# A transformer block with routed experts on one core: the second product of an expert block one block later, and two edits to the planner's steps

## The chip, the cores and the metric

The kernel runs on one core of a Trainium2 chip. The core has five engines that work side by side, each through its own queue of instructions in program order: TensorE (PE; its weight loads are shown as PEld), VectorE (DVE), ScalarE (ACT), GpSimd (POOL) and SyncE (SP, here a queue that issues DMAs). Instructions on different engines wait for each other by semaphores. The metric is the device time of one execution in microseconds (us); smaller is better.

## What is computed

The input is x of shape 2 x 2048 x 256 in fp32, that is two batches of 2048 tokens. Four stages are added to it in turn, each on the layer-normed x:

```python
x = x + attention(layernorm(x))     # 16 heads, causal
x = x + moe(layernorm(x))           # first round, f = 0
x = x + mixer(layernorm(x))
x = x + moe(layernorm(x))           # second round, f = 1, same weights

# moe: 8 experts, the best 2 of each token, and a shared expert for all
h = silu(xt @ w1e.T + b1e) * (xt @ w3e.T + b3e)      # per expert, 256 wide
out_e = h @ w2e.T + b2e
y = sum over the token's two experts of gate * out_e
z = silu(xt @ ws1.T + bs1) * (xt @ ws3.T + bs3) @ ws2.T + bs2   # 512 wide

# mixer
delta = softplus(x @ W1.T + b1)
y = x * delta * ((x @ W2.T + b2) . (x @ W3.T + b3))
```

## The kernel before, in words

**Two halves.** The first half (up to about 1120 us) is attention with a schedule written out by hand. The change does not touch it. The second half holds both rounds of the mixture of experts and the mixer between them. Its tokens are cut into 8 chunks of 512 (c = 0 to 7, four for each batch b), and x stays in SBUF in one tile per chunk.

**Routed experts.** `route` (L744) norms a chunk, transposes it and scores the experts. `sort` (L805) gives each of a batch's 4096 pairs of token and expert a slot, so that tokens of one expert lie together in blocks of 128 rows; there are always EB = 39 blocks for each round and batch. `scatter` (L892) writes the normed rows into the DRAM tile XS at these slots with 32 indirect DMAs issued by POOL (L901). `routed` (L1047) then runs the blocks. `combine` (L916) gathers the results from the DRAM tile YS with 8 indirect DMAs of POOL for each chunk (L928), and DVE adds them, weighted, into x (L941). In the second round a chunk that is complete is written out (L950).

**A run of blocks.** There are four runs of `routed`, one for each round f and batch b. In a run a block j goes through these functions:

- `load(j)` (L1065): SP brings the block's 128 rows from XS into a tile `xs` (four buffers).
- `turn(i)` (L1070): PE transposes two things into one PSUM bank: the activated block i (`es`) and the loaded block i + 4 (`xs`). ACT copies the bank to a tile `turned` (L1083, three buffers).
- `up(j)` (L1085): PE makes the first product `eu` of block j from `turned[j-4]`; DVE adds the bias into `ea` (L1098); ACT takes silu of one half into `es` (L1100).
- `gate(j)` (L1103): DVE multiplies `es` by the other half of `ea` (L1106).
- `down(j)` (L1109): PE makes the second product `ed` from `turned[j]` (L1117); DVE adds the bias into `ey` (L1123, two buffers); SP stores it to YS (L1124).

The loop at L1138 joins them. In iteration i it issues `up(i + 1)`, `down(i - 2)`, `turn(i - 1)`, `load(i + 7)` and `gate(i + 1)`. Calls outside 0 to EB - 1 do nothing.

**Shared expert.** `shared(f, c)` (L1008) takes a chunk through the first two products (`s`, L1019, 16 matmul instructions), silu on ACT (L1021), a multiply on DVE (L1024), the third product (`sy`, L1036, 16 instructions) and an add into x on DVE (L1042).

**Mixer.** `mixer(c)` (L954) norms and transposes a chunk, multiplies by the joined weights (`psz`, L969) and builds softplus from an absolute value (L981), an exponential (L982), an add on POOL (L984), a logarithm on ACT (L992) and several steps on DVE and POOL.

**PSUM.** The banks `ab` (four, for `eu`, the transposes of `turn`, and `s`), `py` (two, for `ed` and `sy`) and `px` (two, for the other transposes, routing and mixer).

**The planner.** The order of all this on each engine is fixed when the program is built. Every work function is a generator. It yields a step as a tuple of estimated costs in us for (DVE, ACT, PE, POOL) around the instructions that it issues. The loop at L1222 takes turns between two main streams, one run of `routed` ("experts") and one chunk of `shared` ("share"), one step each. It adds a step's PE cost to the plan's clock `free[2]`, and the other costs to the clocks of their engines. After each main step `beside()` (L1186) issues steps of three side streams, `moving` (scatters and combines), `mixing` (mixers) and `routing`, as long as the engines that a side step needs are planned to be free within a lead (LEAD, L1181) of the PE clock and its own predecessor is planned to be done (AHEAD). So a side step's place depends on the PE time that the main steps claim.

In a mixer and in the other side streams the tuple yielded comes before the instructions that it stands for; in `routed` and `shared` it comes after them.

A run of experts starts when its scatter is planned to be through (`placed`). A shared chunk starts when its transposed input is there and one of two things holds: all XTS = 3 tiles for transposed inputs are in use, or no expert run is open or ready:

```python
            wait = "experts" in mains or (todo and todo[0] in placed)
            if fit and (live[0] >= XTS or not wait):
```

Of the kernel before, what the change touches and what calls it, by code (L numbers as in the profile page):

```python
# [35 lines left out]
EB = (TOPK * N + E * (P - 1)) // P  # L36
# [15 lines left out]
def hybrid_block(  # L52
# [87 lines left out]
    with tc.tile_pool(name="aw", bufs=1) as aw, ExitStack() as aw_ctx:  # L140
# [109 lines left out]
        with ExitStack() as ac:  # L250
# [303 lines left out]
            while na < len(units) or due or behind:  # L554
# [12 lines left out]
                if run_m:  # L567
# [13 lines left out]
                    kc, i = mx.pick(cols)  # L581
# [108 lines left out]
    def side_bank(nm):  # L690
        return ps_x.tile([P, CH], F32, tag="px", name=nm)
# [8 lines left out]
    def feature_major(nm):  # L700
        while live[0] >= XTS:
            yield None
        live[0] += 1
        return cw.tile([P, 2, CH], F32, tag="xT", name=f"xT_{nm}", bufs=XTS)

    def token_major(nm):
        while held[0] >= XNS:
            yield None
        held[0] += 1
        return cw.tile([P, NB, D], F32, tag="xn", name=f"xn_{nm}", bufs=XNS)  # L710
# [23 lines left out]
    def flipped(xn, xT, nm):  # L734
        yield (0, 1.2, 0.9, 0)
        for d in range(2):
            ps = side_bank(f"flip_{nm}_{d}")
            for i in range(NB):
                nc.tensor.transpose(
                    ps[:, i * P:(i + 1) * P], xn[:, i, d * P:(d + 1) * P], ident  # L740
                )
            nc.scalar.copy(xT[:, d, :], ps)
# [211 lines left out]
    def mixer(c):  # L954

        while c not in joined or (0, c) not in added:
            yield None
        xc = X[c]
        xn = yield from token_major(f"b{c}")
        yield from normed(xc, xn, f"b{c}")  # L960
        xT = yield from feature_major(f"b{c}")
        yield from flipped(xn, xT, f"b{c}")
        z = cw.tile([P, NB, NZ], F32, tag="z", name=f"z_{c}")
        for i in range(NB):
            if i % 2 == 0:
                yield (0.9, 0, 2.0, 0)
            ps = side_bank(f"psz_{c}_{i}")
            for d in range(2):
                nc.tensor.matmul(  # L969
                    ps[:, :NZ], xT[:, d, i * P:(i + 1) * P], wz_s[:, d, :],  # L970
                    start=d == 0, stop=d == 1,
                )
            nc.vector.tensor_add(z[:, i, :], ps[:, :NZ], bz_s)
        live[0] -= 1
        zz = z[:, :, 0:D]


        t = cw.tile([P, NB, D], F32, tag="spt", name=f"spt_{c}")
        u = cw.tile([P, NB, D], F32, tag="spu", name=f"spu_{c}")
        yield (0, 2.0, 0, 0)  # L980
        nc.scalar.activation(t, zz, AF.Abs)  # L981
        nc.scalar.activation(t, t, AF.Exp, scale=-1.0)  # L982
        yield (0, 0, 0, 1.3)
        nc.gpsimd.tensor_scalar_add(u, t, 1.0)  # L984
        bcm = small.tile([P, NB, NS], F32, tag="bcm", name=f"bcm_{c}", bufs=2)
        bc = small.tile([P, NB], F32, tag="bc", name=f"bc_{c}", bufs=2)
        yield (1.5, 0, 0, 0)
        nc.vector.tensor_mul(bcm, z[:, :, D:D + NS], z[:, :, D + NS:])
        nc.vector.reduce_sum(bc, bcm, axis=AX.X)
        nc.vector.scalar_tensor_tensor(t, u, 1.0, t, ALU.subtract, ALU.subtract)  # L990
        yield (0, 1.0, 0, 0)
        nc.scalar.activation(u, u, AF.Ln)  # L992
        yield (0, 0, 0, 2.5)
        nc.gpsimd.tensor_tensor(u, u, t, ALU.subtract)
        yield (1.2, 0, 0, 0)
        nc.vector.scalar_tensor_tensor(u, zz, 0.0, u, ALU.max, ALU.add)
        yield (0, 0, 0, 2.5)
        nc.gpsimd.tensor_tensor(xn, xn, u, ALU.mult)
        for h in range(2):
            yield (1.0, 0, 0, 0)  # L1000
            for i in range(2 * h, 2 * h + 2):
                nc.vector.scalar_tensor_tensor(
                    xc[:, i, :], xn[:, i, :], bc[:, i:i + 1], xc[:, i, :], ALU.mult, ALU.add
                )
        mixed.add(c)
        held[0] -= 1
# [40 lines left out]
    def routed(f, b):  # L1047

        xs, turned, h, reg = {}, {}, {}, {}
        nm = f"{f}_{b}"  # L1050
        ws = {
            e: [
                nc.values_load(
                    words[f, b][0:1, w:w + 1], engines=[e], min_val=0, max_val=8 ** FW - 1,
                    skip_runtime_bounds_check_because="words of eight experts",
                )
                for w in range(WORDS)
            ]
            for e in (mybir.EngineType.PE, mybir.EngineType.DVE)
        }  # L1060

        def expert(j, eng):
            return (ws[eng][j // FW] >> (3 * (j % FW))) & (E - 1)

        def load(j):  # L1065
            if j < EB and j not in xs:
                xs[j] = ew.tile([P, D], F32, tag="xs", name=f"xs_{nm}_{j}", bufs=4)
                nc.sync.dma_start(xs[j], XS[b][j * P:(j + 1) * P, :])

        def turn(i):  # L1070

            halves = [t for t in ((h.pop(i, None), 0), (xs.pop(i + 4, None), 1)) if t[0] is not None]
            if not halves:
                return
            ps = ps_ab.tile([P, 2, D], F32, tag="ab", name=f"tr_{nm}_{i}")
            for t, k in halves:
                for d in range(2):
                    nc.tensor.transpose(  # L1078
                        ps[:, k, d * P:(d + 1) * P], t[:, d * P:(d + 1) * P], ident
                    )  # L1080
            turned[i] = ew.tile([P, 2, D], F32, tag="turned", name=f"turned_{nm}_{i}", bufs=3)
            a, z = halves[0][1], halves[-1][1] + 1
            nc.scalar.copy(turned[i][:, a:z, :], ps[:, a:z, :])  # L1083

        def up(j):  # L1085
            if j >= EB:
                return
            v = expert(j, mybir.EngineType.PE) * WE
            o = expert(j, mybir.EngineType.DVE) * BE
            ps = ps_ab.tile([P, CH], F32, tag="ab", name=f"eu_{nm}_{j}")  # L1090
            t = turned[j - 4]
            for d in range(2):
                nc.tensor.matmul(  # L1093
                    ps, t[:, 1, d * P:(d + 1) * P], we_s[:, bass.ds(v + d * CH, CH)],
                    start=d == 0, stop=d == 1,
                )
            a = ew.tile([P, CH], F32, tag="ea", name=f"ea_{nm}_{j}", bufs=2)
            nc.vector.tensor_add(a, ps, be_s[:, bass.ds(o, CH)])  # L1098
            t = ew.tile([P, D], F32, tag="es", name=f"es_{nm}_{j}", bufs=3)
            nc.scalar.activation(t, a[:, 0:D], AF.Silu)  # L1100
            h[j] = (t, a)

        def gate(j):  # L1103
            if j < EB:
                t, a = h[j]
                nc.vector.tensor_tensor(t, t, a[:, D:], ALU.mult)  # L1106
                h[j] = t

        def down(j):  # L1109
            if j < 0:  # L1110
                return
            v = expert(j, mybir.EngineType.PE) * WE
            o = expert(j, mybir.EngineType.DVE) * BE
            ps = ps_y.tile([P, CH], F32, tag="py", name=f"ed_{nm}_{j}")
            t = turned[j]
            for d in range(2):
                nc.tensor.matmul(  # L1117
                    ps[:, 0:D], t[:, 0, d * P:(d + 1) * P],
                    we_s[:, bass.ds(v + 2 * CH + d * D, D)],
                    start=d == 0, stop=d == 1,  # L1120
                )
            y = ew.tile([P, D], F32, tag="ey", name=f"ey_{nm}_{j}", bufs=2)
            nc.vector.tensor_add(y, ps[:, 0:D], be_s[:, bass.ds(o + CH, D)])  # L1123
            nc.sync.dma_start(YS[b][j * P:(j + 1) * P, :], y)  # L1124

        for j in range(4):
            load(j)
        yield (0, 0, 2.5, 0)
        for j in range(4):
            turn(j - 4)  # L1130
            load(j + 4)
            if j == 1:
                yield (0, 0.8, 0.5, 0)
                up(0)
                yield (0.7, 0.45, 1.72, 0)
        yield (0.4, 0.9, 0.5, 0)
        gate(0)
        for i in range(EB + 2):  # L1138
            up(i + 1)
            yield (0.7, 0.45, 1.72, 0)  # L1140
            down(i - 2)
            if i > 0:
                turn(i - 1)
            load(i + 7)
            yield (0.4, 0.6, 1.3, 0)
            gate(i + 1)
            yield (0.42, 0, 0, 0)
        ran.add((f, b))


# [23 lines left out]
    def mixing():  # L1174
        for c in range(TC):
            yield from mixer(c)
# [141 lines left out]
```

## Time and profile before

The time is the median of 3 runs. The profile is one execution by itself; its span is from its first to its last instruction.

| what | value |
|---|---|
| time, median of 3 runs | 2194.92 us (2192.74 to 2195.27) |
| profiled execution, its own time | 2195.39 us |
| its span | 2193.7 us |
| mean granted clock of TensorE | 0.964 |
| scatters (32 indirect stores of POOL, first to last) | from 1212.6, 1320.9, 1669.7 and 1946.4 us, some 42 to 45 us each |
| last second product `ed` of the program | 2139.2 to 2140.3 us |
| first and last gather behind it | 2143.5 and 2187.4 us (end of the last) |

How it is read: a row of a group or of the timeline names the line of the kernel, the engine, the operation and its tiles (out<-in), how often, and how long. "idle before" is the time in which the engine had nothing to run just before that instruction, with the one that released it. "remote" stands for an unknown releaser. In the timeline the first two columns are start and duration in us, and neighbouring instructions of one kind are merged. A stretch's row gives the busy time of each engine in it. PE counts each matmul of the program as two records here.

### The profile page before, as it was taken

How to read it: one execution, taken by the hardware profiler on the slowest of the kernel's cores; microseconds unless marked ns; L12 is line 12 of the kernel's file. 1: busy time of each engine (PE TensorE's matmuls, PEld its weight loads, DVE VectorE, ACT ScalarE, POOL GpSimd, SP SyncE). 2: the span in 40 equal slices, each digit the busy share in tenths (PEclk: the TensorE clock that was granted, in tenths of full speed). 3: DMA queues.
4: the chain of work that ended last, by engine and by line, in shares of the span. 5: the costliest groups of instructions: out<-in, count | busy, mean ns of one | idle time of the engine just before them, and what ended most of it. 6: DMA issues, size and time to landing. Idle time of an engine off the chain costs nothing.

```text
span 2193.7 us, 36069 instructions
## 1 busy us (share of the span) xinstructions
PE 2018.5 (92%) x11840; PEld 1077.3 (49%) x11840; DVE 1358.3 (62%) x3428; ACT 1064.1 (49%) x1566; POOL 870.1 (40%) x1153
## 2 busy tenths in 40 slices
PE   6999999999999999999989995999998799987993
PEld 4444444444444444444446563656664456654662
DVE  4767776777667777678515462447775277652643
ACT  1567477577767677678851121323442144421330
POOL 3434344254344444344451716025235352343305
PEclk8999999999999999999999997999999899998997
DMA  3211110000000000000013212233101241012523
GB/s 95 72 39 57 33 32 7 8 6 4 9 4 6 4 4 6 4 4 1 3 53 160 80 49 92 87 100 98 58 25 68 74 121 61 22 63 75 178 79 120
DMA packets 87602, 113.03 MB, mean 52 GB/s; under 512 B 16384, under 2 KB 75136, under 8 KB 87296
## 3 DMA queue, kind: packets, MB, share of 16 engines
q1 hardware_dynamic: 73488, 75.08, 10.8%
q0 software_dynamic: 12288, 33.57, 4.6%
q8 instruction: 101, 1.65, 0.3%
q10 hardware_dynamic: 1648, 2.10, 0.3%
q14 instruction: 77, 0.63, 0.1%
HBM read 54.59 MB, written 51.64 MB: 48 GB/s over the span
## 4 chain that ended last, share of the span: by engine, by line
PE 79%; DVE 6%; issue 4%; another core or an unknown queue 4%; ACT 3%; POOL 2%; DMA 1%; DVEq 0%; SPq 0%; ACTq 0%; POOLq 0%
PE st L394 15%; PE o L413 12%; PE psm L344 12%; PE eu L1093 10%; PE s L1019 8%; PE ed L1117 5%; PE sy L1036 4%; PE psk L278 3%; PE tr L1078 2%; PE psv L304 1%; PE psj L462 1%; PE psz L969 1%; PE psl L769 1%; POOL yg L928 1%
## 5 line engine op out<-in xcount | busy, mean ns | idle before, releaser
L398 ACT ACTIVATE pt<-st 128x1024 f32<-128x1024 f32 (+3 forms) x640 | 551.9, 896 | 177.3 <-PE psm L344 130.6
L344 PE MATMUL psm<-kT,qT 32*128 32x512 f32 (+3 forms) x2560 | 611.0, 564 | 8.6 <-DMA kT<-sk 4.2
L394 PE MATMUL st<-qT,kT 32*128 32x512 f32 (+3 forms) x2560 | 592.1, 554 | 3.0 <-ACT pt L398 2.9
L358 DVE TENSOR_REDUCE part<-psm 128x1 f32<-128x512 f32 x768 | 478.3, 683 | 148.9 <-PE psm L344 144.0
L424 POOL TENSOR_TENSOR oa<-oa,op 128x512 f32<-128x512 f32 (+3 forms) x288 | 313.5, 1089 | 408.2 <-ACT op L422 406.3
L394 PEld LDWEIGHTS st<-qT,kT 32*128 32x128 f32 x2560 | 251.1, 184 | 214.6 <-ACT pt L398 137.8
L344 PEld LDWEIGHTS psm<-kT,qT 32*128 32x128 f32 x2560 | 272.2, 185 | 84.9 <-issue 33.0
L413 PE MATMUL o<-pt,v 128*32 128x512 f32 (+3 forms) x2560 | 301.5, 541 | 12.9 <-DVE part L358 5.5
L353 DVE CUSTOM_DVE_ANT_0 junk<-psm,maskq 128x512 bf16<-128x512 f32 (+3 forms) x512 | 224.1, 487 | 76.5 <-PE psm L344 58.9
L1093 PE MATMUL eu<-we,turned 128*128 x560 | 264.8, 595 | 0.0
L1100 ACT ACTIVATE es<-ea 128x256 f32<-128x256 f32 x156 | 65.0, 417 | 390.1 <-DVE ea L1098 337.4
L1019 PE MATMUL s<-xT_f,ws 128*128 128x512 f32 x512 | 238.1, 609 | 11.6 <-DVE hsh L1024 6.1
L928 POOL DMA_INDIRECT yg<-ys,slot x128 | 128.5, 1004 | 301.6 <-issue 105.9
L1117 PE MATMUL ed<-we,turned 128*128 x624 | 166.1, 389 | 40.2 <-ACT turned L1083 14.5
L1098 DVE TENSOR_TENSOR ea<-eu,be 128x512 f32<-128x512 f32 x156 | 107.5, 689 | 131.0 <-PE eu L1093 97.5
L401 POOL TENSOR_SCALAR_AFFINE_SELECT pt<-pt 128x256 f32<-128x256 f32 x256 | 103.1, 408 | 213.2 <-ACT pt L398 210.9
L422 ACT COPY op<-o 128x512 f32<-128x512 f32 (+3 forms) x288 | 148.9, 517 | 77.1 <-PE o L413 66.9
L1117 PEld LDWEIGHTS ed<-we,turned 128*128 128x128 f32 x624 | 118.0, 193 | 115.9 <-issue 62.5
L1036 PE MATMUL sy<-ws,hsh 128*128 128x256 f32 x512 | 126.0, 396 | 39.3 <-DVE hsh L1024 19.7
L413 PEld LDWEIGHTS o<-pt,v 128*32 128x32 f32 x2560 | 53.1, 108 | 217.6 <-DVE part L358 79.4
L901 POOL DMA_INDIRECT xs<-xn_f,slot x128 | 124.8, 975 | 85.9 <-DVE slot L855 42.6
L1019 PEld LDWEIGHTS s<-xT_f,ws 128*128 128x128 f32 x512 | 96.4, 195 | 117.6 <-issue 99.0
(268 smaller groups left out, 2085.7 us busy)
## 6 DMA issues: line engine op xcount, KB each, us to landing
xs<-xs SPq DMA_DIRECT2D x156, 128.0 KB
ys<-ey SPq DMA_DIRECT2D x156, 128.0 KB
xs<-zeros SPq DMA_DIRECT2D x78, 128.0 KB
we<-in_we_dram SPq DMA_DIRECT2D x8, 768.0 KB
kT<-sk SPq DMA_DIRECT2D x128, 32.0 KB
out_dram<-x SPq DMA_DIRECT2D x8, 512.0 KB
x<-in_x_dram SPq DMA_DIRECT2D x6, 512.0 KB
be<-in_be_dram SPq DMA_DIRECT2D x1, 3072.0 KB
```

The lines of the kernel that those rows point to most:

```text
L344: nc.tensor.matmul(ps[:, :n], self.q[r, i * P:(i + 1) * P], kT[b, g, kc][r, :n], start=True, stop=True,)
L353: nc.vector.tensor_tensor_reduce(junk[j % 2][:, :n], ps[:, :n], maskq[:, CH - n:], 1.0, LOW, ALU.add, ALU.max, m,)
L358: nc.vector.reduce_max(m, ps[:, :n], axis=AX.X)
L394: nc.tensor.matmul(st[:, i, off:], k[r, ks], q[r, off:], start=True, stop=True)
L398: nc.scalar.activation(pt[:, :, off:], st[:, :, off:], AF.Exp)
L413: nc.tensor.matmul(o[32 * j:32 * j + 32, off:], V[kb // NB][:, kb % NB, 4 * g + j, :], pts[j // 2][:, j % 2, off:], start=True, stop=True,)
L424: nc.gpsimd.tensor_tensor(a[:, off:], a[:, off:], t[:, off:], ALU.add)
L928: nc.gpsimd.indirect_dma_start(out=y, out_offset=None, in_=YS[b], in_offset=bass.IndirectOffsetOnAxis(ap=slots[f, b][:, k, n:n + 1], axis=0),)
L1019: nc.tensor.matmul(ps, w[:, d, cs], xT[:, d, :], start=d == 0, stop=d == 1)
L1036: nc.tensor.matmul(ps[:, k, :], h[d][:, i * P:(i + 1) * P], ws2_s[:, d, :], start=d == 0, stop=d == 3,)
L1093: nc.tensor.matmul(ps, t[:, 1, d * P:(d + 1) * P], we_s[:, bass.ds(v + d * CH, CH)], start=d == 0, stop=d == 1,)
L1117: nc.tensor.matmul(ps[:, 0:D], t[:, 0, d * P:(d + 1) * P], we_s[:, bass.ds(v + 2 * CH + d * D, D)], start=d == 0, stop=d == 1,)
```

## The change

There are two places. In `mixer` one step that covered two ACT instructions becomes two steps of 1.1 us each in the plan, one before the absolute value and one before the exponential.

In `routed` the second product moves from `down(i - 2)` to `down(i - 3)`, so block j's second product is issued in iteration j + 3 and not j + 2, and the loop gets one more iteration to finish. Three steps of the loop now depend on what the iteration holds: the step behind `up` is yielded only if there was a first product; the step behind `load` claims 0.86 us of PE and no ACT once i is over EB; `gate` and its step are left out when no block i + 1 exists.

```diff
@@ -977,8 +977,9 @@
         t = cw.tile([P, NB, D], F32, tag="spt", name=f"spt_{c}")
         u = cw.tile([P, NB, D], F32, tag="spu", name=f"spu_{c}")
-        yield (0, 2.0, 0, 0)
+        yield (0, 1.1, 0, 0)
         nc.scalar.activation(t, zz, AF.Abs)
+        yield (0, 1.1, 0, 0)
         nc.scalar.activation(t, t, AF.Exp, scale=-1.0)
@@ -1135,16 +1136,21 @@
-        for i in range(EB + 2):
+        for i in range(EB + 3):
             up(i + 1)
-            yield (0.7, 0.45, 1.72, 0)
-            down(i - 2)
+            if i + 1 < EB:
+                yield (0.7, 0.45, 1.72, 0)
+            down(i - 3)
             if i > 0:
                 turn(i - 1)
             load(i + 7)
-            yield (0.4, 0.6, 1.3, 0)
-            gate(i + 1)
-            yield (0.42, 0, 0, 0)
+            if i <= EB:
+                yield (0.4, 0.6, 1.3, 0)
+            else:
+                yield (0.4, 0, 0.86, 0)
+            if i + 1 < EB:
+                gate(i + 1)
+                yield (0.42, 0, 0, 0)
         ran.add((f, b))
```

## The prediction

> **What bounds the kernel now.** I read the busy shares first, then the stretches of the second half, then who PE waits for, and last the end of the timeline.
>
> ```profile
> span 2193.7 us, 36069 instructions
> PE 2018.5 (92%) x11840; PEld 1077.3 (49%) x11840; DVE 1358.3 (62%) x3428; ACT 1064.1 (49%) x1566; POOL 870.1 (40%) x1153
> ```
>
> PE is the bound: no other engine is busy for two thirds of the span. The change touches only what runs after attention, so only 1120 to 2194 us counts. There the records of PE leave 108 us of gaps up to its last matmul at 2160.9. The waits of PE say whose they are:
>
> ```profile
> PE sy L1036 <- DVE hsh L1024: 19.7, 4, 13.2
> PE sy L1036 <- issue: 15.4, 1, 15.4
> PE ed L1117 <- ACT turned L1083: 14.5, 16, 1.7
> PE ed L1117 <- DVE x L1042: 13.8, 1, 13.8
> PE ed L1117 <- DVE ey L1123: 11.9, 1, 11.9
> ```
>
> The columns are total us, times, longest. The third line is what the change aims at: sixteen short stops, none over 1.7 us. The others are few and long. In the timeline they lie in four places, each the later part of a scatter (32 indirect stores on POOL). The stretches before, in and after the last scatter, and the end (columns: stretch, length, busy us of PE, PEld, DVE, ACT, POOL, granted clock, DMA share, GB/s):
>
> ```profile
> 1946.00:1968.00 22.00, 18.15 (x55) 9.37 (x53) 8.12 (x25) 5.71 (x9) 18.04 (x34) 1.00 0.27 107
> 1968.00:1992.00 24.00, 5.40 (x12) 3.50 (x12) 1.99 (x4) 0.87 (x2) 15.76 (x30) 0.57 0.22 87
> 1992.00:2140.00 148.00, 146.25 (x558) 92.49 (x559) 76.25 (x159) 42.77 (x88) 31.84 (x32) 0.99 0.37 114
> 2140.00:2194.00 54.00, 20.93 (x66) 12.07 (x64) 19.86 (x39) 2.75 (x4) 31.18 (x32) 0.72 0.40 120
> ```
>
> In 1968 to 1992 PE, DVE and ACT stand almost still together while POOL issues; summed over the four scatters such gaps of PE are 5.1 + 25.7 + 21.7 + 22.7 = 75 us. Between 1992 and 2140 PE has 1.75 us of gap: the last run of expert blocks is purely PE's. After 2140 the end is POOL's: 32 gathers behind the last block. PE works only 20.9 us of these 54:
>
> ```profile
> 2139.16 1.13 PE L1117 MATMUL ed<-we,turned 128*128 x4 [0.52 <-ACT turned L1083]
> 2140.13 13.90 PE L1019 MATMUL s<-xT_f,ws 128*128 128x512 f32 x32
> 2153.86 7.07 PE L1036 MATMUL sy<-ws,hsh 128*128 128x256 f32 x32
> ```
>
> So the last shared chunk (`s`, `sy`; 2140.1 to 2160.9, 20.8 us) runs free of charge beside the gathers. Whatever PE does **before** the last `ed` sets the end; what it does after costs nothing.
>
> **The change part by part.** No instruction is added or taken away; the planner runs when the program is built, so the new order can be read off it.
>
> *1. Second product three blocks behind.* A typical stop (start us, us, engine, line; ACT is in `Abs`, table load, `Exp` when the copy of the transposes comes due):
>
> ```profile
> 1774.51 1.06 ACT L981 ACTIVATE spt<-z 128x1024 f32<-128x1024 f32 x1 [1.35 <-DVE z L973]
> 1775.58 1.28 ACT L982 ACT_TABLE_LOAD   x1
> 1776.88 1.06 ACT L982 ACTIVATE spt<-spt 128x1024 f32<-128x1024 f32 x1
> 1777.84 0.57 ACT L1083 COPY turned<-tr 128x512 f32<-128x512 f32 x1
> 1778.46 1.13 PE L1117 MATMUL ed<-we,turned 128*128 x4 [1.52 <-ACT turned L1083]
> ```
>
> The copy landed at 1778.4; `ed` could have gone at 1776.9. With `ed` a block later (blocks follow every 3.0 us: `eu` starts at 1440.71 and 1443.73) the copy has 1.5 us to spare. The stops at the tail of two runs (0.52 us, six times) go too: behind the last `eu` the order becomes ed35 tr37 ed36 tr38 ed37 ed38, so one `ed` (0.86) always stands between a transpose and its user. Ends: -14.5 us, all of it; -6 us, if the busy ACT then stops the next reader (PSUM `ab` has four banks, so `tr` two blocks on waits for this copy; the activated `es` is late as well). Nearest row for that: the transposes of `es` waited only 2.4 us in all, in a scatter. I take **-12**. What moves with `ed`: its bias add on DVE (0.42 us) and its store on SP, past one block's `ea`, gate and load. Each comes no later after its own `ed`. The `xs` load queued behind the store on SP waits as before; no new wait. At the tail `ey` has two buffers and a store takes under 2.8 us (2140.8, end of the last `ey`, to the first gather at 2143.5), while the last `ed` come 0.9 to 1.2 us apart: up to 1 us, inside the range. The extra iteration holds only ed38 and adds no work.
>
> *2. Fewer counted steps in the tail.* The old tail books 3 x (1.72 + 1.3) = 9.06 us of PE, the new one 1.3 + 1.3 + 0.86 + 0.86 = 4.32. A scatter is booked at 32 x 1.3 = 41.6 us of POOL. With a slower-running plan clock, the last scatter is "placed" only after s_1_6 and sy_6 are emitted; no expert run is open or ready then, so the planner starts the last shared chunk instead of holding it back. In the new order 6 of its 16 `s` instructions precede the first transpose of the last expert run, the rest precede its fourth `eu`; **nothing follows the last `ed`**. Its 20.8 us come out from behind the gathers. Was PE waiting there, so that it fills a hole? Before, PE reached that place with the data there: after the scatter it still did sy_5, two `ed` and s_1_6, and it did not stop again. So high end and value **+20.8**; low end +8, if the stall in the scatter reaches into the moved chunk. In exchange the gathers run alone: in the trace they take 2143.5 to 2187.4 = 43.9 us, with five pauses longer by 0.1 to 0.8 us and slower issues, most for `x` adds queued on DVE behind the chunk's `hsh`; undisturbed they come every 1.253 us, 32 x 1.253 = 40.1: **-3.8** (ends -3.8 and 0).
>
> *3. Abs as its own step.* The rule that speaks against it is in the Trainium skill, "ScalarE: Activation LUTs", Table sets: batch activations by set, since a switch costs 2.66 us, 1.28 load and 1.38 drain. The row shows 1.28 and no drain: `Exp` starts 0.02 after its load. Had the split added a load to each of 8 mixers, ACT would pay 8 x 1.3 = 10 us by the row, 21 by the rule. But the page also has `abs` in every set, and the built program has 41 loads before and after. So **0**: ACT is under half busy, and POOL's add on `Exp` may come about 1 us later (on POOL itself only five rows of the mixers change places, none past a scatter). If that cover fails (side chain late for the next scatter): 8 us, in the range.
>
> *4. The scatter stalls.* 75 us tied to scatters which the change leaves, but at other points of PE's stream: the second round's first scatter about a block earlier, its last about 4 us of PE work later. The trace has a mild case (5 us: PE had independent shared products) and a hard one (25.7). **0**, ends -10 and +10.
>
> Sum: -12 + 20.8 - 3.8 + 0 + 0 = **+5.0**. The profiled execution took 2195.39 us around its span of 2193.7, so 2200.4; it lies 0.5 over the median of the runs, 2194.92, so I predict **2199.9**.
>
> **The rivals.** *Filled hole, faster* (0.22): the last scatter's stall is long enough that the moved chunk runs inside it. It decides once PE reaches s_1_7 some 8 us before the stall ends. The first scatter speaks for it: there shared products ran on while ACT waited. Against: 11 us of tail and 21 of s_1_6 and sy_6 come first. Then 20.8 falls to 8: 2187. *Stops come back* (0.15): `tr` and `eu` inherit ACT's lateness, part 1 yields 6 or less: 2206. *Worse scatter stalls* (0.17): products needing ACT or DVE for every block fall into the windows, +10: 2210. That the change does not do what it says is ruled out by the order: `ed` j stands behind `eu` j+4.
>
> **How the numbers follow.** Forecast 0.46, own range 2195 to 2205. A measurement of this kernel tells about 0.2%, 4.4 us, from no change: the line is 2199.3. Slower: 0.22 of the forecast, 0.13 of stops coming back, 0.17 of worse stalls: 0.52. Same: 0.21 of the forecast, 0.02 of stops coming back, 0.07 of the filled hole: 0.30. Faster: the other 0.15 of the filled hole, 0.03 of the forecast: 0.18. Range 2187 to 2211.
>
> **What would show it.** Right: PE's wait for `turned` near zero; no `s` or `sy` after the last `ed`; that `ed` some 9 us later, near 2149; 50 us from it to the end instead of 53.5. Wrong: the last `ed` before 2140 (hole filled), new PE waits of `tr` or `eu` on ACT, or scatter gaps far from 75 us.

## The result: slower by 0.9%, and the profile after

| what | before | changed |
|---|---|---|
| time, median of the runs side by side | 2194.51 us (2192.74 to 2195.27, 4 runs) | 2213.11 us (2207.32 to 2220.08, 4 runs) |
| profiled execution, its own time | 2195.39 us | 2207.32 us |
| its span | 2193.7 us | 2205.6 us |
| end of attention: first transpose `flip_f` behind it | 1145.6 us | 1137.85 us |
| span from there to the end | 1048.05 us | 1067.73 us |
| last `ed` starts / from there to the end | 2139.16 / 54.5 us | 2154.94 / 50.65 us |

The ratio is 1.0093, with a 95% interval of 1.007 to 1.0116. The forecast was +5.0 us; the medians say +18.6. The profiled execution of the changed kernel is the shortest of its four, and its first half, which no edit touches, ended 7.75 us earlier than in the other trace. So the two traces are compared from the first `flip_f` (L739) on, and there they differ by 19.7 us, which fits the medians. Times "from the flip" below are counted from that instruction. In the changed kernel lines behind the mixer are one higher, so the `eu` of L1093 is on L1094.

PE's waits in the changed kernel (columns: total us, times, longest):

```profile
PE ed L1118 <- issue: 34.4, 2, 21.5
PE sy L1037 <- DVE hsh L1025: 20.5, 7, 13.6
PE ed L1118 <- DVE x L1043: 12.7, 1, 12.7
...
PE eu L1094 <- ACT turned L1084: 5.6, 6, 2.1
...
PE tr_-4_13758 L1079 <- DMA xs<-xs: 4.5, 1, 4.5
```

The sixteen stops of `ed` for `turned` (14.5 us) are gone. In their place `eu`, the next reader of the same tile, stops six times for 5.6 us. The first three lines are for the most part the long waits in the scatters. All gaps of PE behind the flip are 98.7 us, 97.9 before: the saving is not there. Sorted, they are 5.6 us for `turned` (14.5 before), 4.5 for `xs` (3.1), 78.3 in the scatters (75.5) and 10.2 in short waits elsewhere (4.8).

The stretches before, in and behind the last scatter, and the end (columns as before: stretch, length, PE, PEld, DVE, ACT, POOL, granted clock, DMA share, GB/s):

```profile
1942.60:1957.00 14.40, 12.47 (x39) 6.64 (x38) 7.99 (x23) 5.83 (x9) 11.93 (x23) 1.00 0.28 109
1957.00:1989.00 32.00, 6.12 (x23) 4.52 (x23) 1.75 (x5) 0.74 (x2) 21.81 (x42) 0.60 0.24 95
1989.00:2156.00 167.00, 166.97 (x620) 104.92 (x620) 80.05 (x164) 44.79 (x90) 31.62 (x32) 0.98 0.33 101
2156.00:2205.60 49.60, 0.00 (x0) 0.00 (x0) 15.99 (x33) 0.00 (x0) 30.35 (x32) 0.52 0.43 132
```

In the second row PE stands still again, for longer than before. In the third it has no gap and is busy for all 167 us. In the last it has nothing left to do: the moved chunk is no longer behind the last `ed`, and the gathers run alone at even steps, as the start of POOL's timeline there shows (start, length, and the idle time before):

```profile
2159.56 0.95 POOL L928 DMA_INDIRECT yg<-ys,slot  x1 [76.49 <-issue]
2160.81 0.94 POOL L928 DMA_INDIRECT yg<-ys,slot  x1 [0.31 <-issue]
2162.06 0.95 POOL L928 DMA_INDIRECT yg<-ys,slot  x1 [0.30 <-issue]
```

The 19.7 us split at two instants. PE goes on behind the last scatter 846.6 us from the flip before and 851.0 after: **+4.4**. From there to the start of the last `ed` it takes 147.0 and 166.1 us: **+19.1**, about the chunk of 20.8 less three tail stops of 0.52. From that `ed` to the end: **-3.8**. So behind the last scatter everything came as worked out. Ahead of it 13.0 us of stops for `turned` were taken away and 5.6 came back, and yet PE passed it 4 us later.

### The profile page after: what moved, and what is told of

Same layout as the page of the kernel before. It is cut to its first block, busy times and chain, and to the rows that moved or that the text cites. A ratio compares the mean times of both kernels' runs of the same rounds, so it can differ in the third digit from the quotient of the medians.

```text
span 2205.6 us, 36068 instructions
## 1 busy us (share of the span) xinstructions
PE 2012.0 (91%) x11840; PEld 1074.5 (49%) x11840; DVE 1356.3 (61%) x3428; ACT 1062.6 (48%) x1566; POOL 872.4 (40%) x1153
## 4 chain that ended last, share of the span: by engine, by line
PE 77%; DVE 7%; another core or an unknown queue 5%; issue 4%; ACT 3%; DMA 2%; POOL 2%; DVEq 0%; SPq 0%; POOLq 0%; ACTq 0%
PE st L394 15%; PE o L413 12%; PE psm L344 12%; PE eu L1094 10%; PE s L1020 7%; PE ed L1118 5%; PE sy L1037 4%; PE psk L278 3%; PE tr L1079 2%; PE psz L969 1%; PE psj L462 1%; PE psv L304 1%; DMA yg<-ys,slot 1%; PE psl L769 1%
## 5 line engine op out<-in xcount | busy, mean ns | idle before, releaser
L413 PE MATMUL o<-pt,v 128*32 128x512 f32 (+3 forms) x2560 | 301.5, 541 | 12.9 <-DVE part L358 5.5
L1094 PE MATMUL eu<-we,turned 128*128 x560 | 270.8, 607 | 6.8 <-ACT turned L1084 5.6
```

Source lines behind the costliest of these rows:

```text
L413: nc.tensor.matmul(o[32 * j:32 * j + 32, off:], V[kb // NB][:, kb % NB, 4 * g + j, :], pts[j // 2][:, j % 2, off:], start=True, stop=True,)
L1094: nc.tensor.matmul(ps, t[:, 1, d * P:(d + 1) * P], we_s[:, bass.ds(v + d * CH, CH)], start=d == 0, stop=d == 1,)
```

## The experiments

Each expectation names its theories as they stood before the run. The question was first whether the chunk is the loss (e1 to e8), then where the saved stops went (e9 to e17). Ratios stand against the kernel before on the same chip at the same time. The runs fell on different chips, and from e9 on this became the finding: on two of the chips the kernel before takes 2110 us and not 2190.

| run | what it is | before, us | ratio | 95% |
|---|---|---|---|---|
| e1 | changed, last chunk held back | 2188.6 | 1.0028 | 1.0005 to 1.005 |
| e2 | before + lag of three | 2188.6 | 1.0000 | 0.9986 to 1.0015 |
| e3 | before + chunk moved ahead | 2188.6 | 1.0077 | 1.0055 to 1.0099 |
| e4 | before + Abs step | 2188.6 | 1.0118 | 1.0097 to 1.014 |
| e5 | changed, last two chunks held | 2192.6 | 0.9994 | 0.9982 to 1.0007 |
| e6 | before, last two chunks held | 2192.6 | 0.9978 | 0.9968 to 0.9989 |
| e7 | before + uncounted steps | 2192.6 | 1.0080 | 1.0064 to 1.0097 |
| e8 | changed | 2192.6 | 1.0101 | 1.0076 to 1.0125 |
| e9 | before + lag + Abs step | 2110.2 | 1.0011 | 0.9997 to 1.0025 |
| e10 | before + lag + uncounted steps | 2110.2 | 0.9933 | 0.9919 to 0.9946 |
| e11 | before + lag, two chunks held | 2110.2 | 1.0004 | 0.9991 to 1.0016 |
| e12 | changed | 2109.6 | 1.0042 | 1.0026 to 1.0057 |
| e13 | before + lag | 2109.6 | 0.9996 | 0.9982 to 1.0009 |
| e14 | as e10 | 2109.6 | 0.9946 | 0.9926 to 0.9966 |
| e15 | before, for its trace (one run, 2112.64 us) | 2109.6 | | |
| e16 | as e10 | 2188.3 | 1.0009 | 0.9998 to 1.002 |
| e17 | as e1 | 2188.3 | 1.0025 | 1.0012 to 1.0039 |

### The place of the last chunk: e1, e3, e17

e1 and e17 are the changed kernel with the last shared chunk held until no expert run is open or due:

```diff
-            if fit and (live[0] >= XTS or not wait):
+            last = fit[0] in [(1, c) for c in range(TC - 1, TC)] if fit else False
+            last = last and ("experts" in mains or bool(todo))
+            if fit and not last and (live[0] >= XTS or not wait):
```

e3 does the opposite to the kernel before:

```diff
-            if fit and (live[0] >= XTS or not wait):
+            if fit and (live[0] >= XTS or not wait or fit[0] == (1, TC - 1)):
```

> The changed kernel, with one thing undone: the last shared chunk may not start while an expert run is open or due, so its 32 instructions follow the last `ed` again. Theory A (the moved chunk is the whole loss: 20.8 us of PE work less 3.8 us of calmer gathers, and the removed stops are worth about nothing): 17 us under the changed kernel's 2213, near 2196. Theory B (the new lag and order cost by themselves, the chunk little): 2205 or more. Theory C (the removed stops are worth their 12 us and the scatters merely drew badly): 2184.

> The kernel before with nothing changed but the start of the last shared chunk: it is let in while the last expert run is open, so that nothing follows the last `ed`. Theory A and C: plus 17 us, 2211. Theory B: under 2203.

> The changed kernel with the last shared chunk held behind the last ed. Kernel before near 2190 us (stalls): ratio 1.000 to 1.004 as in e1. Kernel before near 2110 us (no stalls): the changed kernel's 1.0042 less 17 us (20.8 of the chunk, 3.8 given back by the gathers), ratio 0.996; if the changed kernel lost by something else than the chunk: 1.000 or more.

Holding it takes the changed kernel from 1.0093 to 1.0028 in the first pair and from 1.0101 to 1.0025 in the second: 14 and 17 us of 2190 (each ratio is against the kernel before on its own chip; the two of a pair ran on different chips). Moving it ahead in the kernel before costs 0.77%, 17 us (12 to 22). The forecast's net for this step was 20.8 - 3.8 = 17.0. **The chunk is shown, and its size.** What is left over, 1.0028 and 1.0025, is +5 us by the medians in both runs (2193.81 against 2188.6, 2193.34 against 2188.33; 3 to 9 us by the interval of e17), where the forecast had -12.

### The parts alone: e2, e4, e7, and e8

e2 has `EB + 3` and `down(i - 3)` in the old loop and no other edit. e4 has only the second `yield (0, 1.1, 0, 0)`. e7 keeps the lag of two and leaves out the steps without a first product. e8 is the changed kernel once more.

> The kernel before with the lag of three blocks alone (one more iteration, all steps counted as before, one step for Abs and Exp). In its order the last shared chunk stays behind the last `ed`. Theory A: within 4 us of before, 2190 to 2198, with PE's 14.5 us of waits for `turned` at `ed` gone and about as much new waiting elsewhere. Theory B: 2200 or more. Theory C: 2182.

> The kernel before with only Abs as a step of its own. That alone shifts the plan so far that the last shared chunk is again started ahead of the last expert run. Theory A and C: 2211, by the chunk. Theory B: within 4 us of before, since the lag is as it was.

> The kernel before with only the uncounted steps of the tail (the lag stays at two, one step for Abs and Exp). In its order the last shared chunk is again ahead of the last expert run. Theory A: plus 17 us over before, as in the run with the chunk alone. Theory B (the loss of the changed kernel needs the lag): within 4 us of before.

> The changed kernel as it is, once more, on one chip with the others and with a second profile. Theory A: 17 to 20 us over before, and in the profile the time from the first transpose behind attention to the last `ed` within 5 us of the first profile's 1017; the difference between its profiles lies in attention and in the scatters.

e8 gives the result again: from the flip to the end 1068.9 us, 1.2 more than the first trace. e2 brings the stops for `turned` down to 1.0 us and gains nothing: 1.0000, and by its interval at most 3 us. e4 and e7 each lose as much as the whole change, since in both built orders the last chunk stands ahead of the last run, while `ed` still stops for `turned` (15.75 and 12.9 us). That corrects a reading: the forecast put the chunk's move down to the uncounted steps. Built with lag alone, lag and Abs, or lag and uncounted steps, the plan leaves the chunk last; with Abs alone, uncounted steps alone, or all three, it moves it. The plan sits at a threshold, and each edit can tip it.

### Two chunks held: e5 and e6

The same edit with `TC - 2`: the last two chunks wait behind the last `ed`, e5 in the changed kernel, e6 in the one before.

> The changed kernel with the last two shared chunks held back until no expert run is open or due, so 64 instructions (41.6 us of PE) follow the last `ed`, in the shadow of the gathers. Theory A (what PE does before the last `ed` sets the end): 12 us under e1, that is some 6 us under before of the same chip: minus 20.8, plus some 4 us for a wait at the start of the last run, whose filler is gone, plus some 4 us for gathers disturbed longer. Theory B (the chunks ahead of the last run fill a hole that PE has there anyway): within 4 us of e1.

> The kernel before with the last two shared chunks held back. Theory A: 12 us under before. Theory B: within 4 us of before.

If one chunk runs free beside the gathers, a second might. e6 gains 4.8 us (0.22%), less than half of what was hoped, and e5 lies some 7 us under e1 by the ratios, where 12 were hoped. In e6 the last `ed` starts 15.7 us earlier from the flip, but from there to the end it takes 65 us instead of 54.5. POOL's gathers there show why:

```profile
2144.19 0.95 POOL L928 DMA_INDIRECT yg<-ys,slot  x1 [0.30 <-issue]
2149.84 1.07 POOL L928 DMA_INDIRECT yg<-ys,slot  x1 [4.70 <-DVE x L941]
```

A gather needs one of four `yg` tiles, which DVE's add into x (L941) sets free; with two chunks on DVE the adds come later, here by 4.7 us. More tiles were not tried.

### Where the saved stops go: e9 to e15, on chips without the stalls

> The kernel before with the second product three blocks behind and the absolute value as its own step, steps counted as before; the built order leaves the last shared chunk at the end, behind the last ed. It differs from the lag alone (span 2186.7, waits of eu for turned 0.97 us) by the Abs step only. Theory A (the Abs step puts ACT's copies late behind es and the table load, and so the saved stops come back at eu): waits of PE for turned 5 to 6 us as in the changed kernel, almost all at eu, and 3 to 6 us above the lag alone, ratio 1.001 to 1.003. Theory B (the uncounted tail steps move the side work so that the copies come late): waits for turned 1 us or less, ratio 1.000.

> The changed kernel with the absolute value put back into one step with the exponential; the built order then leaves the last shared chunk at the end. Theory A (the Abs step brings the stops back): waits of eu for turned 1 us or less, about as long as the kernel before or the lag alone, ratio 0.998 to 1.001, that is 18 us under the changed kernel since the chunk is back behind the last ed as well. Theory B (the tail steps bring them back): waits for turned 5 to 6 us, ratio 1.001 to 1.004. If the tail steps alone made the loss whatever the place of the chunk: ratio 1.008.

> The kernel before with the lag of three blocks alone and the last two shared chunks held behind the last ed. If gains add up: lag alone gave 0, two chunks held gave -4.8 us, so -5 us, ratio 0.998. If the lag's saved stops are only eaten by what falls into the last scatter there (the run's start waits 5.3 us for xs in the lag alone), holding the chunks moves that place and up to 5 us more come out: ratio 0.995 to 0.996. If the gathers behind the last ed are the bound by then: ratio 0.998 or a little more.

> The changed kernel beside the kernel before once more. If the chip shows the scatter stalls (kernel before near 2190 us): ratio 1.008 to 1.011 as before. If it does not (kernel before near 2110 us): theory S (the saved stops were given back inside the scatter stalls): the moved chunk costs 20.8 - 3.8 = 17, the lag with uncounted steps gains 15.5 (e10), so ratio 1.001; theory A (the Abs step gives them back): 17 to 19 us more than before, ratio 1.008 to 1.009.

> The kernel before with the second product three blocks behind, and nothing else. With stalls: ratio 1.000 as in e2. Without stalls: theory S and theory A both: the 14.5 us of stops come out less up to 6 us of waits of runs' starts for xs, ratio 0.994 to 0.997; if e10's gain came from the uncounted steps and not from the lag: ratio 1.000.

> The changed kernel with the absolute value put back into the step of the exponential; the built order has the last shared chunk behind the last ed. With stalls: theory A ratio 0.993 to 0.996 (the gain of e10 is there as well), theory S 0.998 to 1.001 (the stalls eat it). Without stalls: 0.993 as in e10.

> The kernel before, for its trace on the same chip. With stalls: gaps of PE in the four scatters 70 to 80 us, stops of ed for turned 14 to 15 us. Without: gaps in the scatters under 10 us, the stops of ed for turned still 13 to 16 us.

The kernel before takes 2110 us on these two chips, 80 less. Its trace (e15) says which 80. The windows before and in the last scatter of e15, columns as above:

```profile
1884.30:1900.00 15.70, 15.70 (x45) 7.85 (x44) 8.64 (x25) 6.40 (x10) 13.06 (x25) 1.00 0.28 110
1900.00:1925.00 25.00, 25.00 (x88) 15.96 (x87) 6.39 (x10) 3.49 (x6) 20.62 (x40) 1.00 0.31 120
```

The second row is the place where PE did 5.4 us of work in 24 on the other chip. Here it does 25 of 25, at full clock, while POOL issues the same stores. The 75 us of gaps in the four scatters are absent, and from the flip to the end it takes 965.5 us instead of 1048.05. Of these 82.5 us, 69.4 are gaps of PE (the stalls, less 6.1 of new waits, below) and 12.9 are busy time of PE: 904.0 us behind the flip, at a mean granted clock of 0.99 up to its last product, against 916.9 at 0.95. So the program alone does not make the stalls. That makes a clean bench for the rest. PE's waits in e15:

```profile
PE ed L1117 <- ACT turned L1083: 14.5, 16, 1.7
...
PE tr_-4_13758 L1078 <- DMA xs<-xs: 3.1, 1, 3.1
...
PE tr_-4_17533 L1078 <- DMA xs<-xs: 2.8, 1, 2.8
PE tr_-4_15659 L1078 <- DMA xs<-xs: 2.2, 1, 2.2
...
PE tr_-3_17540 L1078 <- DMA xs<-xs: 1.1, 1, 1.1
```

The stops are the same 14.5 us. New are the last three waits for `xs`: at a run's start the first rows have not come out of the scatter when PE asks for them. With the 3.1 of the second run, which the other chip has too, they are 9.2 us.

**The lag alone** (e13) gains nothing here either (0.9996; both theories had 0.994 to 0.997, and 1.000 stood for a gain that comes from the uncounted steps). Its waits show where the gain stays:

```profile
PE tr_-4_15623 L1078 <- DMA xs<-xs: 8.8, 1, 8.8
...
PE tr_-4_13758 L1078 <- DMA xs<-xs: 4.6, 1, 4.6
...
PE tr_-4_17519 L1078 <- DMA xs<-xs: 3.5, 1, 3.5
...
PE eu L1093 <- ACT turned L1083: 1.7, 3, 0.7
PE tr_-3_15630 L1078 <- DMA xs<-xs: 1.1, 1, 1.1
...
PE tr_-3_17526 L1078 <- DMA xs<-xs: 0.6, 1, 0.6
```

Stops for `turned` fall from 14.5 to 1.7, waits for `xs` rise from 9.2 to 18.7. PE reaches the starts of the runs sooner, and the scatters do not end sooner in step. In the third run, which has 7.7 of the 9.5 us, there is a second reason. When PE asks for the first rows there, it has done the first products of 10.0 shared chunks; in e15 it has done 10.9. So the lag alone moves a piece of the plan as well, 14 `s` instructions or 12 us of cover, from ahead of the run's start to behind it.

**Lag and uncounted steps** (e14; e10 is the same kernel) gain 11 and 14 us. No theory of e10 had that; the best was 0.998.

```profile
PE tr_-4_13758 L1078 <- DMA xs<-xs: 4.8, 1, 4.8
...
PE eu L1093 <- ACT turned L1083: 1.8, 4, 0.8
```

The waits for `xs` are 4.8 us, all at the second run's start, because this plan has the 12 us of shared work ahead of the third run again (10.9 chunks): there the first `ed` comes 549.7 us from the flip, 25.7 behind the end of its scatter; in e13 it comes 538.2 us from it, only 16.8 behind. The forecast gave the uncounted steps no effect but the chunk's move. On these chips they are what turns the lag into time.

**With the Abs step as well** it is the changed kernel (e12). Its ratio, 1.0042, lies between the two theories (1.001, and 1.008 to 1.009). In the traces 953.2 becomes 972.6 us from the flip, +19.3. The chunk has moved again (17 of it), and the stops for `turned` are back:

```profile
PE eu L1094 <- ACT turned L1084: 6.4, 8, 2.1
```

In e14 this row is 1.8. e9 against e13, where the chunk stays last in both, says the same: 1.7 without the Abs step (above), and with it:

```profile
PE eu L1094 <- ACT turned L1084: 5.0, 5, 2.1
```

The ratios of these two, 1.0011 and 0.9996 on two chips, have intervals that overlap. DVE's waits name the link. In the changed kernel, then in e14:

```profile
DVE spt L991 <- POOL spu L985: 20.8, 7, 5.1
```

```profile
DVE spt L990 <- POOL spu L984: 5.8, 4, 1.4
```

In the mixers DVE waits 17 to 21 us for POOL's add on the exponential with the Abs step (the changed kernel, e9, e12), and 5 to 7 without (before, e13, e14, e15). One place in the timeline of the changed kernel, all engines, in order of time:

```profile
1542.48 0.42 ACT L1101 ACTIVATE es<-ea 128x256 f32<-128x256 f32 x1 [2.36 <-DVE ea L1099]
...
1542.91 1.28 ACT L983 ACT_TABLE_LOAD   x1
...
1544.21 1.06 ACT L983 ACTIVATE spt<-spt 128x1024 f32<-128x1024 f32 x1
...
1545.43 2.78 POOL L985 TENSOR_SCALAR spu<-spt 128x1024 f32<-128x1024 f32 x1 [3.87 <-ACT spt L983]
...
1548.25 1.23 DVE L991 SCALAR_TENSOR_TENSOR spt<-spu,spt 128x1024 f32<-128x1024 f32 x1 [5.09 <-POOL spu L985]
...
1549.72 0.68 DVE L1099 TENSOR_TENSOR ea<-eu,be 128x512 f32<-128x512 f32 x1
...
1550.44 0.42 ACT L1101 ACTIVATE es<-ea 128x256 f32<-128x256 f32 x1 [2.43 <-DVE ea L1099]
...
1550.88 1.28 ACT L993 ACT_TABLE_LOAD   x1
...
1552.17 1.06 ACT L993 ACTIVATE spu<-spu 128x1024 f32<-128x1024 f32 x1
...
1553.14 0.57 ACT L1084 COPY turned<-tr 128x512 f32<-128x512 f32 x1
...
1553.76 3.68 PE L1094 MATMUL eu<-we,turned 128*128 x4 [2.15 <-ACT turned L1084]
```

The exponential stands behind an expert's silu; POOL's add (L985) follows it, and DVE's mixer step (L991) waits 5.1 us for that. Behind it in DVE's queue stands the bias add of an expert block (`ea`), behind that the silu `es` on ACT, then the logarithm with its table load, then the copy `turned`. PE's `eu` gets that copy 2.15 us late. Three of the six stops in this trace, 4.4 of the 5.6 us, have this chain; none of the four in e14 has it. A step of the side chain moved by a few instructions has stopped the main chain through a queue that both share.

e11 adds nothing (1.0004, where 0.995 to 0.998 was hoped): its waits for `xs` are 27.7 us, 13.6 of them at the start of the last run, where a chunk that covered the scatter now lies behind.

### The same kernel where the stalls are: e16

> The changed kernel with the absolute value back in the step of the exponential (last shared chunk behind the last ed). Kernel before near 2110 us (no stalls): ratio 0.993 to 0.996 as in e10 and e14. Kernel before near 2190 us (stalls): theory S (PE goes on when the scatter has ended, so what is saved ahead of it is lost): 0.997 to 1.001; theory A (the Abs step alone had taken the gain): 0.993 to 0.996.

The kernel that gains 0.54 and 0.67% on the chips without the stalls gives 1.0009 here, with an upper and a lower end within 0.2%. The difference, 0.0063 to 0.0076 of 2190, is 14 to 17 us. So where the stalls are the gain is gone, and the Abs step alone did not take it: without it nothing is gained either. With it and the chunk held (e17) the ratio is 0.16% or 3.5 us higher, but the intervals of e16 and e17 overlap. That the stalls, and nothing else in which the chips differ, take the gain is argued; this kernel ran on one chip that has them.

How they could take it can be read in part. Times from the flip, in us, of the last scatter:

| kernel | first store | last store ends | PE goes on | PE idle in it |
|---|---|---|---|---|
| before | 800.8 | 843.1 | 846.6 | 22.7 |
| changed | 804.8 | 848.5 | 851.0 | 27.8 |
| e16 | 787.9 | 828.6 | 834.4 | 23.7 |
| before, no stalls (e15) | 738.9 | 779.3 | | 3.9, for `xs` |
| changed, no stalls (e12) | 742.1 | 782.4 | | 0 |

In all twelve traces with stalls PE goes on 3.0 to 6.4 us behind the end of the second and third scatter, however far it had come. Behind the fourth it is 2.4 to 5.8 us in nine of them, 0.4 in e6, and 11 in e4 and e7, where PE's next `s` waits for ACT. Time saved ahead of a scatter then counts, as a rule, only as far as the scatter itself comes earlier. That this accounts for all 14 us is not shown. A rival stands untested, PE's speed: in e2's trace PE's gaps are 5.4 us shorter than in the kernel before and its busy time 6.0 us longer (922.9, at a granted clock of 0.94); in e16's the busy time is 2.9 shorter. Single traces with stalls differ too much: e1 and e17 are one kernel, with 1046.0 and 1051.4 us from the flip to the end. In e16's own trace the last scatter even ends 14.5 us earlier than in that of the kernel before, which ran on another chip; its second half there is 7.5 us shorter, while the medians of 20 and 30 runs on one chip say no change.

## Why the prediction was wrong

**What bounds the kernel** held: what follows the last `ed` is POOL's, what precedes it is PE's. Of the signs of being right, 50 us from the last `ed` to the end and no `s` or `sy` behind it came true. But that `ed` came 23.5 us later from the flip, where +8.8 was the sum, and waits of `eu` for ACT, a sign of being wrong, were there.

**Part 2 held.** +20.8 and -3.8 were both measured: behind the last scatter +19.1 with the three tail stops taken off, at the end -3.8, and by the ratios 14 to 17 us for the step. Its reason was too narrow (any of several edits tips the plan), and it missed that the uncounted steps also put back the shared work that the lag alone takes from ahead of a run's start.

**Part 1 is the step that failed**: "I take -12". The stops of `ed` did go, all 14.5 us. The row was right and the step from it to the sum was not: stops of PE are not time of the kernel until what PE does next comes earlier too. What the runs showed in place of the -12, on chips with stalls like that of the result, is 0 for the lag alone (e2, whose plan moves the same 12 us of shared work as e13) and +5 for all parts but the chunk (e1, e17). In the two traces of the result PE's gaps gave it all back: 5.6 us at `eu`, 1.4 for `xs`, 2.8 in the scatters, 5.4 in short waits elsewhere. With lag and uncounted steps the time does fall by 11 to 14 us where there are no stalls (e10, e14), and by nothing where there are: 1.0009 of 2190 is +2 (e16). The Abs step, with 3.3 and 4.6 us of stops come back at `eu` (e9 against e13, e12 against e14), may add the 3.5 that would make this the +5; that is not clear of the noise.

On the chips without stalls the traces of e12 and e15 close: PE's gaps fall by 7.4 us (-8.0 for `turned`, -4.0 for `xs`, +4.6 elsewhere), its busy time by 2.5, and from PE's last product to the end it takes 17.0 longer. That is +7.1 from the flip, and by the ratio it is +9 (5.5 to 12). The forecast of +5.0 lies just below that, by a sum with other terms.

**Part 3**, "0", was right about the table loads (the traces have 42 before and after) and wrong about the cover. ACT under half busy hides the instruction, but DVE's queue behind POOL's add does not hide the delay: 3.3 and 4.6 us of stops.

**Part 4**, "0, ends -10 and +10", asked whether the stalls would grow. Their sum hardly did: 75.5 before, 78.3 after, five more in the last, two less in the first. The question left out was whether a saving ahead of a stall outlasts it. On the chip where that was tried it does not: the 14 to 17 us between e10, e14 and e16. PE going on just behind a scatter's end fits that, but the traces do not follow it to the last us, and the cause stays open.

**Rivals.** "Stops come back" (+6 for part 1 at most, 2206) and "worse scatter stalls" (2210) each had a piece, 5.6 us at `eu` and 2.8 in the scatters; neither has the 5.4 us of short waits elsewhere. The range, which let only one of the two happen, ended 2 us short. The filled hole is out: PE had no gap from the moved chunk's start on.

**A version better than both.** The changed kernel without the Abs step: 0.9933 and 0.9946 where there are no stalls, 1.0009 where there are. With stalls the best was the kernel before with two chunks held, 0.9978.

## What to carry to other kernels

A stop that the waits list against the bounding engine is worth its time only if that engine's next appointment moves too. Before counting it, find the next point that something else sets (here a run's start, set by a scatter that POOL issues) and ask whether that comes earlier. And where a planner fixes the order, build each edit alone and look at where the large pieces end up, since any small edit may tip one of them across the point that sets the end.

## What was not expected of the hardware

Whether PE, DVE and ACT stand still in a burst of 32 indirect stores of POOL depends on the chip: 75 us of gaps in the traces where the kernel before takes 2190 us, none of them on the two chips where it takes 2110. The stores keep their pace in both, 40.3 to 45.7 us for each scatter. In the second scatter PE's first stop comes 16.3 us behind the first store in all twelve traces with stalls. The Trainium skill ("SBUF — State Buffer", "SBUF: two separate sides") says that a DMA cannot be slowed by a compute operation and vice versa, and leaves a port that GpSimd and DVE share as a place where the two can meet; here engines stood during DMAs that POOL issued, though no run shows by what they were held. Waiting for instructions to be fetched does not explain the third scatter of the kernel before: its trace has no packet of an instruction queue from 3.9 us behind the first store until 12 us behind the end of the last. The cause stays open.

The first half, the same instructions in every kernel here, ends at 1137.7 to 1139.8 us in some executions and at 1144.9 to 1146.3 in the others, on chips of both kinds. A single trace carries this 7 us, so second halves were compared from the flip on.
